# Later norms, two probability tiles, another PSUM pool for the output transposes, and a first attention without VectorE copies

## The chip, the cores and the metric

The kernel runs on one core of a Trainium2 chip. The metric is the device time of one execution in microseconds (us); the time given for a kernel is the median of its runs. TensorE is written PE (and PEld for its weight loads), VectorE DVE, ScalarE ACT, GpSimd POOL, and SyncE, which issues the DMAs here, SP.

## The reference, cut to what matters

The input is 16 sequences of 256 tokens with 128 channels. There are two parts, each behind a layer norm without weights and with a residual around it.

```python
x = x + first_attention(layernorm(x))     # windows of 64 tokens, 16 heads of 8
x = x + six_layers(layernorm(x))

def first_attention(x):
    q, k, v = split(x_windows @ W_qkv)                 # per head
    q, k = layernorm8(q) * g + b, layernorm8(k) * g + b
    return softmax(q @ k.T) @ v @ W_proj + b_proj

def six_layers(x):                         # windows of 32, look back one; 16 heads of 64
    for i in range(6):
        h = shift_tokens(x)
        q, k, v = split(h @ Wqkv[i])
        q, k = rotary(l2norm(q) * qs[i]), rotary(l2norm(k) * ks[i])
        x = local_attention(q, k, v) @ Wo[i] + x
        h = layernorm(shift_tokens(x)) * g[i] + b[i]
        a, gate = split(h @ W1[i] + b1[i])
        x = a * gelu(gate) @ W2[i] + b2[i] + x
    return x
```

`l2norm` divides each head's 64 values by the root of their squares' sum; `layernorm8` works over the 8 values of a head.

## The kernel before

**Order.** The kernel is a Python program that emits instructions; a planner then orders the instructions of each engine by when it believes that they are ready, with the order of the program as priority. In the six layers PE's order is pinned: `mul` and `flip` (L290 to L294) chain each matmul and transpose behind the one before, so PE runs them as the program emits them, and the others follow. All DMAs touched here are issued by SP, in order.

**First attention (L297 to L547).** Eight units of 512 tokens go through six stages, two steps `k` for a unit, one stage of several units side by side in each step (`merge`). `stage_load` (L364) takes row statistics (`row_stats`, L315: four sums and four sums of squares on ACT, for each of the unit's four tiles) and transposes. `stage_qkv` (L381) projects and normalises q and k. `stage_heads` (L406) splits q and k into a high and a low half-precision part, laid out four times eight values per head: ACT casts the high part (L414), POOL subtracts to get the low part (L415), and DVE copies both into the other two places (L417, L419); then SP transposes the block by DMA (L421). `stage_soft` (L427) makes scores, takes off the maximum on DVE (L448, L449), exponentiates (L459), splits again (L461 on ACT, L462 on POOL) and transposes by DMA (L464). `stage_out` (L467) multiplies probabilities with v for each half `c` of the partitions, into a PSUM tile `po` of its own, takes a reciprocal (L482) and two multiplies (L485) per half, and projects. `stage_norm` (L510) writes the residual to memory and takes the statistics for the second norm by the same `row_stats`. `SPLIT0` (L34) deals the eight PSUM banks to five pools.

**Six layers (L549 to L935).** There are 192 tiles (six layers, 32 tiles of 128 tokens). Each step `t` projects tile `t` (`stage_p`, L632) and does the later stages of tiles before it; `merge_at` (L248) sorts the pieces by their places within the step. `stage_p` has six projections: k in two halves, q in two halves, v in two halves. For a half of k or q DVE multiplies the projection with the rotary table (L643), ACT squares it (L652), DVE sums the squares per head (L653) and POOL adds the rotated parts (L654). After the second half ACT takes logarithm and exponential (L658, L659, through `tab`, whose line in the profile is L275), POOL clips (L660) and multiplies both halves (L664). In the next step PE transposes these halves, four to a bank (`turned`, L608; `project` calls `turn` between its matmuls), and ACT copies them out (L621). The probabilities of a tile go the same way, into one tile `pt` of which there is one buffer; `stage_v` (L765) reads it, in two halves `mb`. PSUM is dealt by `SPLIT` and `USE` (L33, L35): two banks for projections ("p"), four for transposes, feed-forward and more ("t", "w", "f", and half of `stage_v`), two for scores and the other half of `stage_v`. The feed-forward `stage_f` (L837) covers four tiles and is spread over four steps; its gelu needs another table of ACT's, so `tab` and `gelu` (L274, L280) order it against the logarithms and exponentials that come before. In the last layer `emit_out` (L820) transposes the result back, adds the residual of the first part and writes out; it takes its two banks from "p".

Of the kernel before, what the change touches and what calls it, by code (L numbers as in the profile page):

```python
# [33 lines left out]
SPLIT0 = (2, 2, 2, 1, 1)  # L34
# [14 lines left out]
VPRE = 16.0  # L49
# [6 lines left out]
def kernel(  # L56
# [240 lines left out]
    def first_attention(p1, p2, p3, pqp, psp0, pop, pyp, ptp=None):  # L297
# [17 lines left out]
        def row_stats(xt, pre):  # L315
# [3 lines left out]
            for t in range(4):  # L319
                S.activation(sq, xt[:, t], AF.Copy, scale=-1.0 / 128.0, accum_out=mu[:, t : t + 1])  # L320
# [43 lines left out]
        def stage_load(u):  # L364
# [5 lines left out]
            V.tensor_scalar(e.rv, e.rs, VPRE, None, ALU.mult)  # L370
# [35 lines left out]
        def stage_heads(u):  # L406
            e = U[u]
            e.hl = []
            for s in range(2):
                src = e.qk[:, :, s * 128 : s * 128 + 128].rearrange("p t (h d) -> p t h d", d=8)  # L410
                hl = p1.tile([128, 4, 16, 4, 8], HP, name=f"hl{s}")
                for t in range(4):
                    hi, lo = hl[:, t, :, 0], hl[:, t, :, 2 if s else 1]
                    S.copy(hi, src[:, t])  # L414
                    G.tensor_tensor(lo, src[:, t], hi, ALU.subtract)  # L415
                    if s:
                        V.tensor_copy(hl[:, t, :, 1:4:2], hl[:, t, :, 0:3:2])  # L417
                    else:
                        V.tensor_copy(hl[:, t, :, 2:4], hl[:, t, :, 0:2])  # L419
# [47 lines left out]
        def stage_out(u, n2):  # L467
            e = U[u]
            for n in range(2):
# [4 lines left out]
                for c in range(2):  # L474
                    r = slice(64 * c, 64 * c + 64)
                    po = pop.tile([128, 8, 18], F32, name="po")
                    for gm in range(8):
                        p = gm % 4 * 2 + gm // 4
                        for q, (a, b) in enumerate(((0, 0), (0, 1), (1, 0))):
                            T.matmul(po[:, p], pt0[r, a * 8 + gm], v[r, b, p], start=(q == 0), stop=(q == 2))  # L480
                    rc = p3.tile([128, 8], F32, name="rc0")
                    V.reciprocal(rc, po[:, :, 16])  # L482
                    for hp in range(2):
                        h = slice(64 * hp, 64 * hp + 64)
                        V.tensor_tensor(  # L485
                            o0[h, c],
                            po[h, :, hp * 8 : hp * 8 + 8],
                            rc[h].unsqueeze(2).to_broadcast([64, 8, 8]),
                            ALU.mult,
                        )  # L490
# [117 lines left out]
    def turned(src, dst, mb):  # L608
        hold = []

        def one(m):
            if m == 0:
                hold.append(bank("t").rearrange("p (m q) -> p m q", q=128))
            flip(hold[0][:, m], src(m), ident)
            if m == 3:
                to = dst
                if isinstance(dst, Tl):
                    if mb == 0:
                        dst.pt = work.tile([128, 8, 128], F32, name="pt", bufs=1)
                    to = dst.pt  # L620
                S.copy(to[:, mb * 4 : mb * 4 + 4], hold[0])  # L621
# [10 lines left out]
    def stage_p(t):  # L632
        d = tiles[t]
        tq = tqs[d.i]
        d.nat = {}
        for s in (1, 0):
            r = front.tile([128, 16], F32, name="r", bufs=3)
            mcs = []
            for hb in range(2):
# [11 lines left out]
                sq = front.tile([128, 8, 64], F32, name="sq")  # L651
                S.activation(sq, pp.rearrange("p (h d) -> p h d", d=64), AF.Square)  # L652
                V.tensor_reduce(r[:, hb * 8 : hb * 8 + 8], sq, AX.X, ALU.add)  # L653
                G.tensor_tensor(mc, m2[:, :, 0], m2[:, :, 1], ALU.add)  # L654
                mcs.append(mc)
                if hb == 0:
                    yield
            tab(r, r, AF.Ln, bias=tiny)  # L658
            tab(r, r, AF.Exp, scale=-0.5)  # L659
            G.tensor_scalar(r, r, 1e12 / WPRE, None, ALU.min)  # L660
            for hb in range(2):
                mc = mcs[hb]
                rb = r[:, hb * 8 : hb * 8 + 8]
# [4 lines left out]
        for hb in range(2):  # L668
# [5 lines left out]
            if hb == 0:  # L674
                yield
# [346 lines left out]
```

## Time and profile before

| what | value |
|---|---|
| median of three runs | 3215.65 us (3214.28 to 3218.32) |
| profiled execution | 3213.12 us, span 3211.3 us |
| PE busy | 2994.2 us, 93% |
| DVE busy | 2583.3 us, 80% |
| POOL busy | 2510.2 us, 78% |
| ACT busy | 2384.4 us, 74% |
| first projection of the six layers | starts at 268.8 us |

Everything in the profile comes from one profiled execution. Its page gives busy time by engine, the span in 40 slices of 80 us with a digit for the busy tenths, and the costliest groups of instructions. A group is named by line, engine and operation and by what it writes and reads (out<-in); after the bar come busy time, the mean length of one in ns, and the engine's idle time before them with what ended it. A line of the waits reads: engine and instruction that waited, what it waited for, total us, how often, the longest. A matmul's end is modelled, so a busy PE isn't PE at its peak.

### The profile page before, as it was taken

What the parts mean: (1) busy time and instruction counts of PE and PEld (TensorE: products, weight loads), DVE (VectorE), ACT (ScalarE), POOL (GpSimd) and SP (SyncE); (2) the same over time, 40 slices, a digit from 0 to 9 for tenths busy, and PEclk for the clock granted to TensorE, in tenths of its full rate; (3) what the DMA queues carried; (4) which work ended last, traced back from release to release, by engine and by line L of the source; (5) the groups of instructions that cost most, each with busy time, mean ns of one, the idle gap of its engine ahead of it and who ended that gap; (6) DMA issues with size and microseconds to landing.
All of it is one profiled execution on the core that took longest, in us unless ns stands there. A gap on an engine that the chain in (4) does not pass through costs nothing. (4 is left out here: it accounts for less than half of the span.)

```text
span 3211.3 us, 153330 instructions
## 1 busy us (share of the span) xinstructions
PE 2994.2 (93%) x67106; PEld 2099.0 (65%) x67106; DVE 2583.3 (80%) x4850; ACT 2384.4 (74%) x5034; POOL 2510.2 (78%) x2578
## 2 busy tenths in 40 slices
PE   4887999999999999999999999999999999999997
PEld 3655766666666666666666666666666666666664
DVE  7987888887788887788887788887788887787774
ACT  6877777777777777777777777777777777776774
POOL 5656988888888788888788888788888788887772
PEclk6558999999999999999999999999999999999998
DMA  4763545444444434444444444444444444443433
GB/s 109 134 130 86 101 96 106 89 85 88 93 95 107 87 87 88 93 95 105 89 87 86 94 96 104 89 88 84 95 98 103 89 89 81 95 93 91 89 89 71
DMA packets 622945, 302.98 MB, mean 94 GB/s; under 512 B 533446, under 2 KB 545732, under 8 KB 622276
## 3 DMA queue, kind: packets, MB, share of 16 engines
q1 hardware_dynamic: 622276, 293.18, 43.5%
q8 instruction: 528, 8.65, 1.1%
q14 instruction: 141, 1.16, 0.1%
HBM read 22.45 MB, written 4.19 MB: 8 GB/s over the span
## 5 line engine op out<-in xcount | busy, mean ns | idle before, releaser
L291 PE MATMUL bank<-wqkv,xhl 128*128 128x512 f16 x3456 | 1234.4, 380 | 10.0 <-ACT sq L652 9.3
L654 POOL TENSOR_TENSOR sum<-mc 128x512 f32<-128x512 f32 x768 | 995.8, 1300 | 230.4 <-DVE mc L643 211.3
L643 DVE TENSOR_TENSOR mc<-bank,tq 128x1024 f32<-128x1024 f32 x768 | 928.2, 1218 | 148.3 <-PE bank L294 135.4
L664 POOL TENSOR_TENSOR sum<-sum,r 128x512 f32<-128x512 f32 x768 | 796.2, 1058 | 31.9
L653 DVE TENSOR_REDUCE r<-sq 128x8 f32<-128x512 f32 x768 | 520.4, 683 | 277.4 <-ACT sq L652 267.4
L294 PE MATMUL bank<-ident,sum 128*128 128x128 f32 x3072 | 710.5, 273 | 0.0
L796 POOL TENSOR_TENSOR ohl<-of,ohl 128x512 f16<-128x512 f32 x384 | 451.7, 1176 | 211.5 <-ACT ohl L795 210.8
L652 ACT ACTIVATE sq<-bank 128x512 f32<-128x512 f32 x768 | 459.6, 608 | 160.4 <-DVE mc L643 158.7
L294 PEld LDWEIGHTS bank<-ident,sum 128*128 128x128 f32 x3072 | 432.4, 141 | 131.8 <-issue 13.9
L291 PEld LDWEIGHTS <-xhl 128*128 128x128 f16 x3456 | 337.6, 98 | 191.0 <-issue 18.5
L795 ACT CAST ohl<-of 128x512 f16<-128x512 f32 x384 | 237.8, 619 | 269.5 <-DVE of L791 266.8
L291 PE MATMUL bank<-vb,pt 64*32 64x65 f32 x6144 | 376.0, 225 | 50.9 <-ACT p L275 26.4
L291 PEld LDWEIGHTS bank<-vb,pt 64*32 64x32 f32 x6144 | 257.0, 105 | 218.6 <-ACT p L275 75.1
L294 PE MATMUL bank<-ident,p 128*128 128x128 f32 x1536 | 355.0, 273 | 0.1
L291 PE MATMUL bank<-v,pt 64*32 64x65 f32 x6144 | 312.6, 224 | 39.4 <-ACT p L275 17.8
L291 PE MATMUL bank<-vw,pt 64*32 64x65 f32 x12288 | 331.8, 225 | 1.2 <-issue 1.0
L791 DVE TENSOR_TENSOR of<-bank,rc 128x256 f32<-128x256 f32 x768 | 295.4, 416 | 1.7
L291 PE MATMUL bank<-ot,wohl 128*128 128x128 f16 x4608 | 292.0, 220 | 2.0 <-issue 1.1
L291 PEld LDWEIGHTS bank<-kt,qt 64*32 64x32 f32 x24576 | 255.4, 105 | 44.4 <-issue 44.1
L291 PE MATMUL bank<-kt,qt 64*32 64x64 f32 (+1 forms) x24576 | 283.7, 223 | 0.3 <-issue 0.2
L291 PEld LDWEIGHTS bank<-v,pt 64*32 64x32 f32 x6144 | 235.2, 105 | 70.5 <-ACT p L275 33.2
L291 PEld LDWEIGHTS <-wohl 128*128 128x128 f16 x4608 | 259.1, 98 | 21.0 <-issue 3.1
(155 smaller groups left out, 5033.9 us busy)
## 6 DMA issues: line engine op xcount, KB each, us to landing
v<-vb SPq DMA_DIRECT2D x384, 130.0 KB
vw<-vb SPq DMA_DIRECT2D x384, 130.0 KB
vw<-vb SPq DMA_DIRECT2D x576, 65.0 KB
wraw<-in_L_ffn_Wqkv_dram SPq DMA_DIRECT2D x36, 256.0 KB
wraw<-in_L_ffn_Wo_dram SPq DMA_DIRECT2D x12, 256.0 KB
ot<-ohl SPq DMA_TRANSPOSE x192
xt<-in_L_attn_x_dram SPq DMA_DIRECT2D x8, 256.0 KB
r1d<-xt SPq DMA_DIRECT2D x8, 256.0 KB
```

The lines of the kernel that those rows point to most:

```text
L291: pin(T.matmul(*args, **how))
L294: pin(T.transpose(*args))
L643: V.tensor_tensor(prod, p4.unsqueeze(3).to_broadcast([128, 8, 2, 2, 32]), tq[:, s, d.j].unsqueeze(1).to_broadcast([128, 8, 2, 2, 32]), ALU ...
L652: S.activation(sq, pp.rearrange("p (h d) -> p h d", d=64), AF.Square)
L653: V.tensor_reduce(r[:, hb * 8 : hb * 8 + 8], sq, AX.X, ALU.add)
L654: G.tensor_tensor(mc, m2[:, :, 0], m2[:, :, 1], ALU.add)
L664: G.tensor_tensor(mc, mc, rb.unsqueeze(2).to_broadcast([128, 8, 64]), ALU.mult)
L791: V.tensor_tensor(of[:, :, a], po[a][:, :, 0:64], rc.unsqueeze(2).to_broadcast([128, 4, 64]), ALU.mult)
L795: S.copy(ohl[:, 0, h], of)
L796: G.tensor_tensor(ohl[:, 1, h], of, ohl[:, 0, h], ALU.subtract)
```

## The change

It has four parts.

First attention: ACT casts and POOL subtracts with an input that is read twice, so each writes two of the four places, and the DVE copies go. The output matmuls of both halves `c` alternate and write one tile of two banks, with one reciprocal and two multiplies for both. The second row statistics take their means by one DVE reduction and a small POOL multiply; a scaling of four numbers (`rv`) goes from DVE to POOL. The pool of `po` has one buffer of two banks instead of two of one.

Norms: the squares of both halves go into one tile, one DVE reduction sums them, and it is emitted with the logarithm, the exponential and the POOL multiplies after the next projection's instructions.

Probabilities: `pt` is two tiles of four blocks each.

Output: `emit_out` takes its banks from "t".

```diff
-SPLIT0 = (2, 2, 2, 1, 1)
+SPLIT0 = (2, 2, 1, 1, 1)
...
-            for t in range(4):
-                S.activation(sq, xt[:, t], AF.Copy, scale=-1.0 / 128.0, accum_out=mu[:, t : t + 1])
+            if pre == "a":
+                for t in range(4):
+                    S.activation(sq, xt[:, t], AF.Copy, scale=-1.0 / 128.0, accum_out=mu[:, t : t + 1])
+            else:
+                V.tensor_reduce(mu, xt, AX.X, ALU.add)
+                G.tensor_scalar(mu, mu, -1.0 / 128.0, None, ALU.mult)
...
-            V.tensor_scalar(e.rv, e.rs, VPRE, None, ALU.mult)
+            G.tensor_scalar(e.rv, e.rs, VPRE, None, ALU.mult)
...
+                hi, lo = (slice(0, 2), slice(2, 4)) if s else (slice(0, 3, 2), slice(1, 4, 2))
                 for t in range(4):
-                    hi, lo = hl[:, t, :, 0], hl[:, t, :, 2 if s else 1]
-                    S.copy(hi, src[:, t])
-                    G.tensor_tensor(lo, src[:, t], hi, ALU.subtract)
-                    if s:
-                        V.tensor_copy(hl[:, t, :, 1:4:2], hl[:, t, :, 0:3:2])
-                    else:
-                        V.tensor_copy(hl[:, t, :, 2:4], hl[:, t, :, 0:2])
+                    two = src[:, t].unsqueeze(2).to_broadcast([128, 16, 2, 8])
+                    S.copy(hl[:, t, :, hi], two)
+                    G.tensor_tensor(hl[:, t, :, lo], two, hl[:, t, :, hi], ALU.subtract)
...
+                both = pop.tile([128, 2, 512], F32, name="po")
+                po = both[:, :, 0:144].rearrange("p c (m e) -> p c m e", e=18)
+                for gm in range(8):
+                    p = gm % 4 * 2 + gm // 4
+                    for q, (a, b) in enumerate(((0, 0), (0, 1), (1, 0))):
+                        for c in range(2):
+                            r = slice(64 * c, 64 * c + 64)
+                            T.matmul(po[:, c, p], pt0[r, a * 8 + gm], v[r, b, p], start=(q == 0), stop=(q == 2))
+                rc = p3.tile([128, 2, 8], F32, name="rc0")
+                V.reciprocal(rc, po[:, :, :, 16])
+                for hp in range(2):
+                    h = slice(64 * hp, 64 * hp + 64)
+                    V.tensor_tensor(
+                        o0[h],
+                        po[h, :, :, hp * 8 : hp * 8 + 8],
+                        rc[h].unsqueeze(3).to_broadcast([64, 2, 8, 8]),
+                        ALU.mult,
+                    )
...
-                    if mb == 0:
-                        dst.pt = work.tile([128, 8, 128], F32, name="pt", bufs=1)
-                    to = dst.pt
-                S.copy(to[:, mb * 4 : mb * 4 + 4], hold[0])
+                    dst.pt[mb] = work.tile([128, 4, 128], F32, name=f"pt{mb}", bufs=1)
+                    S.copy(dst.pt[mb], hold[0])
+                else:
+                    S.copy(dst[:, mb * 4 : mb * 4 + 4], hold[0])
...
+        late = []
+
+        def norm(r, sq, mcs):
+            V.tensor_reduce(r, sq, AX.X, ALU.add)
+            tab(r, r, AF.Ln, bias=tiny)
+            tab(r, r, AF.Exp, scale=-0.5)
+            G.tensor_scalar(r, r, 1e12 / WPRE, None, ALU.min)
+            for hb, mc in enumerate(mcs):
+                rb = r[:, hb * 8 : hb * 8 + 8]
+                G.tensor_tensor(mc, mc, rb.unsqueeze(2).to_broadcast([128, 8, 64]), ALU.mult)
+
         for s in (1, 0):
             r = front.tile([128, 16], F32, name="r", bufs=3)
+            sq = front.tile([128, 16, 64], F32, name="sq", bufs=2)
...
-                sq = front.tile([128, 8, 64], F32, name="sq")
-                S.activation(sq, pp.rearrange("p (h d) -> p h d", d=64), AF.Square)
-                V.tensor_reduce(r[:, hb * 8 : hb * 8 + 8], sq, AX.X, ALU.add)
+                S.activation(
+                    sq[:, hb * 8 : hb * 8 + 8], pp.rearrange("p (h d) -> p h d", d=64), AF.Square
+                )
                 G.tensor_tensor(mc, m2[:, :, 0], m2[:, :, 1], ALU.add)
                 mcs.append(mc)
-                if hb == 0:
-                    yield
...
+                while late:
+                    norm(*late.pop())
+                yield
+            late.append((r, sq, mcs))
             d.nat[s] = mcs
-            yield
...
+            while late:
+                norm(*late.pop())
             if hb == 0:
                 yield
...
-                        mul(po[a][q, m], d.pt[r, mm, q], vv[s, a][r, mm], start=True, stop=True)
+                        mul(po[a][q, m], d.pt[mb][r, m, q], vv[s, a][r, mm], start=True, stop=True)
...
-            pm = bank("p")[:, 0:256].rearrange("p (t c) -> p t c", c=64)[:, 0:n]
+            pm = bank("t")[:, 0:256].rearrange("p (t c) -> p t c", c=64)[:, 0:n]
```

More of the change, by code (lines that the diff above doesn't have):

```diff
@@ L473, in stage_out @@
                 o0 = p3.tile([128, 2, 8, 8], F32, name="o0")
[L474 to L490, printed above, removed]
+                both = pop.tile([128, 2, 512], F32, name="po")
[16 more added lines that the diff above has]
+                    )
                 yield
@@ L615, in one @@
             if m == 3:
-                to = dst
                 if isinstance(dst, Tl):
-                    if mb == 0:
-                        dst.pt = work.tile([128, 8, 128], F32, name="pt", bufs=1)
-                    to = dst.pt
-                S.copy(to[:, mb * 4 : mb * 4 + 4], hold[0])
+                    dst.pt[mb] = work.tile([128, 4, 128], F32, name=f"pt{mb}", bufs=1)
+                    S.copy(dst.pt[mb], hold[0])
+                else:
+                    S.copy(dst[:, mb * 4 : mb * 4 + 4], hold[0])
         turns.extend((lambda m=m: one(m)) for m in range(4))
@@ L650, in stage_p @@
                 m2 = prod.rearrange("p h f g d -> p h f (g d)")
-                sq = front.tile([128, 8, 64], F32, name="sq")
-                S.activation(sq, pp.rearrange("p (h d) -> p h d", d=64), AF.Square)
-                V.tensor_reduce(r[:, hb * 8 : hb * 8 + 8], sq, AX.X, ALU.add)
+                S.activation(
+                    sq[:, hb * 8 : hb * 8 + 8], pp.rearrange("p (h d) -> p h d", d=64), AF.Square
+                )
                 G.tensor_tensor(mc, m2[:, :, 0], m2[:, :, 1], ALU.add)
                 mcs.append(mc)
-                if hb == 0:
-                    yield
[L658 to L663, printed above, removed]
-                G.tensor_tensor(mc, mc, rb.unsqueeze(2).to_broadcast([128, 8, 64]), ALU.mult)
+                while late:
+                    norm(*late.pop())
+                yield
+            late.append((r, sq, mcs))
             d.nat[s] = mcs
-            yield
         d.vb = vb = vbs[t % NV]
@@ L701, in line_up @@
             d = tiles[t - LAG_P]
+            d.pt = [None, None]
             for mb in range(2):
```

## The prediction

> **What bounds the kernel now.** I read the page's engine totals and 40 slices first, then engine busy by stretch, then each engine's waits.
>
> ```profile
> span 3211.3 us, 153330 instructions
> PE   4887999999999999999999999999999999999997
> DVE  7987888887788887788887788887788887787774
> PEclk6558999999999999999999999999999999999998
> ```
>
> The kernel has two parts. In the first slices (first attention) PE has gaps and its granted clock is about half; after that PE is full. Busy time by stretch (columns PE, PEld, DVE, ACT, POOL, clock, DMA share, GB/s):
>
> ```profile
> 60.00:180.00 120.00, 95.73 (x1632) 72.81 (x1630) 111.19 (x281) 91.40 (x256) 79.77 (x63) 0.51 0.69 129
> 180.00:270.00 90.00, 73.84 (x1246) 54.21 (x1243) 68.66 (x191) 63.22 (x179) 44.20 (x40) 0.50 0.63 120
> 340.00:3150.00 2810.00, 2697.44 (x62047) 1887.41 (x62046) 2283.18 (x4151) 2108.37 (x4285) 2290.46 (x2336) 1.00 0.44 93
> ```
>
> From 60 to 180 us DVE is busy 93%, ahead of PE (80%) and ACT (76%). Over 60 to 270 us DVE works 179.9 of 210 us and the rows of its waits there add up to 23.7: it is the engine that hardly ever rests, so it sets the pace of the first part. Part of that work is stretched. The window around 163 us shows it (start, length, engine):
>
> ```profile
> 162.52 2.13 POOL L462 TENSOR_TENSOR ph<-p,ph 128x1024 f16<-128x1024 f32 x1
> ...
> 163.06 1.68 DVE L419 COPY hl<-hl 128x256 f16<-128x256 f16 x1
> ```
>
> The copy's shortest run is 168 ns; this one took 1.68 us and ended (164.74) just after POOL's instruction did (164.65). The groups of 0 to 300 us (busy, mean ns | idle before):
>
> ```profile
> L485 DVE TENSOR_TENSOR o<-po,rc 64x64 f32<-64x64 f32 x128 | 28.0, 219 | 1.9
> L415 POOL TENSOR_TENSOR hl<-qk,hl 128x128 f16<-128x128 f32 x64 | 25.2, 431 | 2.5 <-ACT hl L414 2.5
> L417 DVE COPY hl<-hl 128x256 f16<-128x256 f16 x32 | 14.5, 468 | 0.2
> L419 DVE COPY hl<-hl 128x256 f16<-128x256 f16 x32 | 13.3, 449 | 5.3 <-POOL hl L415 5.2
> L482 DVE RECIPROCAL rc<-po 128x8 f32<-128x8 f32 x64 | 12.6, 200 | 9.1 <-PE po L480 8.3
> ```
>
> From 340 to 3150 us PE works 96%, and what it still waits for is named:
>
> ```profile
> PE bank L291 <- ACT p L275: 44.2, 166, 2.9
> PE bank L291 <- ACT gt L281: 22.4, 88, 0.3
> PE bank L291 <- ACT pt L621: 21.1, 46, 0.5
> PE bank L294 <- DVE gt L834: 9.4, 6, 1.6
> ```
>
> None of them is the norm. So an edit counts in the main part only where it moves one of these.
>
> **The change part by part.** The sum is against the profiled execution, 3213.1 us (span 3211.3 and 1.8 around it); the median of the runs, 3215.65, lies 2.5 above it.
>
> 1. *First attention, DVE.* Removed: the copies, 14.5 + 13.3 = 27.8 us; 32 of 64 reciprocals, 6.3; 128 multiplies of 64x64 (28.0) become 64 of 64x128, which by the 64x128 row of L817 (about 280 ns) are 17.9, so 10.1; the eight L370 scalings (mean 518 ns), 4.1. Added: eight reductions for the mean, by the 128x512 row of L448 (684 ns) 5.5. Net 27.8 + 6.3 + 10.1 + 4.1 - 5.5 = 42.8 us less DVE work.
>
> On POOL, L415 goes from 128 to 256 elements: rows of 431 ns at 128 and 1176 at 512 (L796) give 1.94 ns an element, so 248 ns x 64 = 15.9 us, plus 16 small ones of 245 ns (L660), 3.9. POOL has 124 of 210 us busy there and takes 20 more; without that cover all 20 would be paid. On ACT the wider cast costs 64 x 107 ns = 6.8 (slope of 294 ns at 128 to 1040 at 1024), and 32 sums of 304 + 191 ns go, 15.8: 9 less.
>
> How much of 42.8 reaches the end? With some 40 off, DVE falls to 140 in that stretch and PE leads with 169.6; PE's weight loads wait a further 19.6 there for the probabilities' transposes, whose number is unchanged. 170 + 19.6 = 189 instead of 210: **21 us**. Bounds: 0 if PE and the transposes already hold the stage, 42.8 if every DVE microsecond counts. I take 21 because PE's row is the nearest next limit.
>
> Its new waits: the attention output now has one two-bank tile, so PE waits for one reciprocal and two multiplies (0.2 + 2 x 0.28 = 0.76 us) of the tile before, with the next scores behind it. Between 0.3 (today's row of PE waiting for L485) and 31 x 0.76 = 24; I take 0, for such groups lie about 6.1 us apart (L525 starts from 113.7 to 285.5 us for eight units: 24.5 a unit, four groups each). The mean now passes DVE and POOL, where a 2.13 us L462 can stand ahead: up to 0.68 + 2.13 + 0.25 - 4 x 0.30 = 1.9 us later, with ACT's exponentials queued behind; 8 x 1.9 = 15 above, -9 below (ACT's saving), 0 taken, as ACT rests 26% there. The L370 scaling behind such an L462 holds L392, L393 and PE's next projection, but on DVE it already ran up to 1521 ns. SP's transposes of hl are released by POOL's last subtraction instead of a later copy; no DMA is added and none changes its place in SP's queue.
>
> The Trainium skill speaks against this: its page GPSIMD Engine Reference, section Engine selection, says that two-input elementwise work belongs on VectorE, GpSimd being about 2x slower. By unstretched copies (64 x 0.17 = 11 us) against 15.9 us more on POOL the move would lose 5 us if the two were equally loaded. The row decides for me: the copies cost 27.8 and POOL has room.
>
> The halves of the output matmuls now alternate between partitions 0-63 and 64-127. The Trainium skill's page TensorEngine Tiling (Array Packing), section Key Properties, says that such tiles run in parallel; by that up to half of L480's 51.7 us of PE, an estimate, would go too. No run here shows it. My sum has nothing for it.
>
> 2. *Norms one projection later.* Per pair of halves two reductions of 683 ns become one of 1210 (the 128x1024 row of L399): 384 x 0.156 = 60 us less DVE work, and DVE's 267.4 us of waiting for L652 goes. On the path this is 0, for PE is at 96% and waits for neither; without that cover it would be the whole gain. POOL's queue already has the multiplies of k (L664) behind the addition of q's first half (this L654), so the later place in the program moves them little:
>
> ```profile
> 1409.89 1.27 POOL L654 TENSOR_TENSOR sum<-mc 128x512 f32<-128x512 f32 x1
> 1411.12 0.25 POOL L660 TENSOR_SCALAR r<-r 128x16 f32<-128x16 f32 x1
> 1411.46 2.05 POOL L664 TENSOR_TENSOR sum<-sum,r 128x512 f32<-128x512 f32 x2
> ```
>
>  What is late next is the logarithm on ACT. It waits for the reduction today, with the gelu's table load queued behind it:
>
> ```profile
> 1414.31 0.31 ACT L275 ACTIVATE r<-r,tiny 128x16 f32<-128x16 f32 x1 [0.81 <-DVE r L653]
> 1414.65 0.22 ACT L275 ACTIVATE r<-r 128x16 f32<-128x16 f32 x1
> 1414.88 1.28 ACT L281 ACT_TABLE_LOAD   x1
> ```
>
> The combined reduction ends 1.21 - 0.69 = 0.52 us later after the second square. That happens in the 46 feed-forward blocks where PE waits for L281: +24 at most. Below, -20: half of the 44.2 that PE waits for L275, if DVE runs ahead. But DVE has 0.16 us (2 x 0.683 - 1.21) to 0.69 us (the first half's reduction) less to do upstream in the same step, more than 0.52 at its best, so I take a quarter of 24, **+6**.
>
> 3. *Probabilities in two tiles.* The copy L621 of the next tile follows PE's flips, which follow the last read on PE itself; the 21.1 us wait for L621 is for a bank of the pool of four. 0, both ways.
>
> 4. *Output transposes in the pool of four.* The wait for L834 (six times, 9.4 us): in a pool of four neither half needs the other's add. **-9.4**; Ends: that, 0 if a later bank of the pool waits in its place, +9.4 if the two extra tiles in its rotation cost as much again.
>
> Sum: -21 + 6 - 9.4 = -24.4. 3213.1 - 24.4 = 3188.7 for the profiled execution; from the median 3215.65 - 24.4 = **3191 us**.
>
> **Rivals.**
> *A, slower: the norm really comes a projection later in POOL's queue.* In one step the q multiply starts at 1447.75 and lasts 1.04; PE's flip of it starts at 1450.77:
>
> ```profile
> 1447.75 2.05 POOL L664 TENSOR_TENSOR sum<-sum,r 128x512 f32<-128x512 f32 x2
> ```
>
> That leaves 1.98 us. A projection slot is 2.5 (projections start from 268.8 to 3148.3 us, 192 tiles of six); with 0.52 it is 3.0, so PE stalls 1.0 us in one step of four: 47 x 1.0 = +48. 3215.65 - 21 - 9.4 + 48 = 3233. It decides from a delay of 1.98 + 30.4/47 = 2.6 us. For: POOL is 82% busy there. Against: the order noted above.
> *B, no change: first attention is held by PE and the transposes.* For: PE 94% in 180 to 210 us at clock 0.5, DMA 0.69. Then 3215.65 + 6 - 9.4 = 3212. Against: PE's own waits there name DVE's L449.
> *C, faster: all DVE time counts and the norm costs nothing:* 3215.65 - 42.8 - 9.4 = 3163. For: DVE's 98% with waits. Against: PE's 169.6.
>
> **How the numbers follow.** Forecast 0.50, own range 3172 to 3208; A 0.20, B 0.14, C 0.16. 0.2% (6.4 us) is about what a measurement of this kernel tells from no change. Faster: 0.49 + 0.16 + a third of B = 0.70; same 0.10; slower 0.20. The range runs from a little below C to A, 3157 to 3233.
>
> **What would show it.** L417 and L419 gone; the first projection, at 268.8 us today, some 20 us earlier, DVE's share in 60 to 180 us below PE's; the L834 wait gone; the L275 and L281 waits within a few us of 44.2 and 22.4. Wrong would be: the first projection where it was (B), PE's flips waiting for L664's successor (A), or new bank waits from another order on ACT.

## The result: 3228.6 us, 0.44% slower

The median of five runs is 3228.61 us (3227.84 to 3231.55), against 3215.65 us for the kernel before beside it. The ratio is 1.0044, with a 95% interval of 1.0029 to 1.0058: the change costs 9 to 19 us where a gain of 24 was forecast. The profiled execution took 3231.55 us, its span 3229.8; it is the longest of the five, so the two profiles lie 18.5 us apart where the medians lie 13.0.

The same lines of the page after, and the busy time by stretch (columns PE, PEld, DVE, ACT, POOL, clock, DMA share, GB/s):

```profile
span 3229.8 us, 152190 instructions
PE   4778999999999999999999999999999999999997
DVE  6887887887788787788787788887788787777774
PEclk9759999999999999999999999999999999999998
```

```profile
60.00:180.00 120.00, 91.87 (x1745) 67.09 (x1741) 100.41 (x211) 95.67 (x245) 88.76 (x73) 0.75 0.76 140
180.00:270.00 90.00, 66.39 (x1160) 44.59 (x1159) 68.11 (x132) 62.73 (x151) 56.69 (x54) 0.57 0.61 111
340.00:3150.00 2810.00, 2672.15 (x61308) 1865.71 (x61307) 2246.29 (x3736) 2095.16 (x4243) 2263.47 (x2308) 1.00 0.44 91
```

From 60 to 180 us DVE is down from 111.2 to 100.4 us and POOL up from 79.8 to 88.8, as the diff says. From 340 to 3150 us DVE works 37 us less, and PE too works 25 us less in the same time: it is idle more often. Where the two parts begin and end is read from the group of the projections (count; shortest, median and longest ns; first to last start). Before:

```profile
L291 PE MATMUL bank<-wqkv,xhl x3456: 376/379/634, 268.8 to 3148.3; 128*128 128x512 f16 x192
```

After:

```profile
L291 PE MATMUL bank<-wqkv,xhl x3456: 376/379/634, 252.7 to 3164.8; 128*128 128x512 f16 x192
```

First attention ends 16.1 us earlier. From the first to the last projection there are now 2912.1 us instead of 2879.5, 32.6 more. What follows the last projection went from 63.0 to 65.0 us. The sum, -16.1 + 32.6 + 2.0, is the 18.5 us between the two spans. Engine busy time over exactly those projections says what the 32.6 consist of. Before:

```profile
268.80:3148.30 2879.50, 2757.42 (x63354) 1927.93 (x63351) 2342.30 (x4247) 2160.45 (x4407) 2355.35 (x2405) 1.00 0.43 93
```

After:

```profile
252.70:3164.80 2912.10, 2763.94 (x63367) 1928.06 (x63361) 2329.97 (x3861) 2168.34 (x4407) 2353.04 (x2401) 1.00 0.43 91
```

PE's idle time (length less busy) grew from 122.1 to 148.2 us, 26 of the 32.6; the rest is busy time. Its waits from 340 to 3150 us after, to be set beside those shown of before:

```profile
PE bank L291 <- ACT p L275: 71.6, 240, 0.6
PE bank L291 <- ACT gt L281: 31.5, 92, 0.4
PE bank L291 <- ACT pt L620: 16.4, 36, 0.5
```

The wait for ACT's attention exponential (L275, tile p) was 40.6 us in that stretch before (the 44.2 of the prediction is the row from 340 to 3170 us), now 71.6; that for the gelu was 22.4, now 31.5. The wait for L834 is gone, as forecast. So ACT is late. What ACT itself waits for ahead of its logarithm (tile r), before:

```profile
ACT r L275 <- DVE r L653: 151.2, 206, 1.8
ACT r L275 <- POOL sum L654: 13.0, 16, 0.8
ACT r L275 <- DVE rc L790: 5.0, 17, 0.3
```

After:

```profile
ACT r L275 <- DVE r L640: 218.3, 196, 2.8
ACT r L275 <- DVE rc L800: 76.2, 139, 0.8
ACT r L275 <- POOL sum L667: 46.0, 33, 1.9
```

That is 169 us in 239 waits before and 341 us in 368 after: of 384 logarithms, nearly every one now waits. Counted over the timeline of the whole profile, where k's and q's take turns, k's logarithm waited 64 times of 192 for 20.8 us before and 190 times for 106.2 after, q's 180 times for 151.5 us and 192 times for 246.5. A piece of the timeline shows both kinds of logarithm, k's and q's (start, length, engine; in brackets the idle time before and its releaser). Before, q's waited 0.81 us in the line that the prediction shows; a k of the kernel before waited for nothing:

```profile
1394.19 0.31 ACT L275 ACTIVATE r<-r,tiny 128x16 f32<-128x16 f32 x1
```

After, k's and q's of one step, with the reduction that q's waits for:

```profile
1394.56 0.31 ACT L275 ACTIVATE r<-r,tiny 128x16 f32<-128x16 f32 x1 [0.39 <-DVE rc L800]
...
1400.16 0.31 ACT L275 ACTIVATE r<-r,tiny 128x16 f32<-128x16 f32 x1 [1.35 <-DVE r L640]
```

```profile
1398.85 1.22 DVE L640 TENSOR_REDUCE r<-sq 128x16 f32<-128x1024 f32 x1 [1.03 <-ACT sq L664]
```

q's wait is 1.35 instead of 0.81 us, 0.54 longer, and k's, which mostly did not wait, now does. DVE stands idle for 1.03 us ahead of the combined reduction: it has nothing left to do and waits for the second square. The work that the combined reduction saves is saved in a pause there (such pauses stand ahead of 175 of the 384).

ACT's order changed as well. The planner sets it, and with the new norms it set it differently. In the same step as the first of these logarithms, the kernel before has the cast of the attention output (tile ohl) behind the two exponentials p:

```profile
1390.31 0.59 ACT L621 COPY kt<-bank 128x512 f32<-128x512 f32 x1 [0.20 <-PE bank L294]
1390.80 1.09 ACT L275 ACTIVATE p<-bank 128x512 f32<-128x512 f32 x2
1391.76 0.63 ACT L795 CAST ohl<-of 128x512 f16<-128x512 f32 x1
```

After, it stands ahead of them:

```profile
1390.62 0.62 ACT L805 CAST ohl<-of 128x512 f16<-128x512 f32 x1 [0.32 <-DVE of L801]
1391.14 0.58 ACT L622 COPY kt<-bank 128x512 f32<-128x512 f32 x1
1391.62 1.09 ACT L275 ACTIVATE p<-bank 128x512 f32<-128x512 f32 x2
```

Between 300 and 3120 us the cast stands ahead of both exponentials in 90 of 187 steps before, and in 140 of 185 after.

### The profile page after: what moved, and what is told of

Same layout as the page of the kernel before. It is cut to its first block, busy times and chain, and to the rows that moved or that the text cites. A ratio compares the mean times of both kernels' runs of the same rounds, so it can differ in the third digit from the quotient of the medians.

```text
span 3229.8 us, 152190 instructions
## 1 busy us (share of the span) xinstructions
PE 2982.5 (92%) x67106; PEld 2080.9 (64%) x67106; DVE 2545.8 (79%) x4306; ACT 2388.9 (74%) x4970; POOL 2528.6 (78%) x2594
## 5 line engine op out<-in xcount | busy, mean ns | idle before, releaser
L656 DVE TENSOR_TENSOR mc<-bank,tq 128x1024 f32<-128x1024 f32 x768 | 938.6, 1222 | 185.8 <-PE bank L294 158.1
L640 DVE TENSOR_REDUCE r<-sq 128x16 f32<-128x1024 f32 x384 | 466.9, 1216 | 201.5 <-ACT sq L664 195.3
L664 ACT ACTIVATE sq<-bank 128x512 f32<-128x512 f32 x768 | 468.6, 613 | 62.7 <-DVE mc L656 60.4
L275 ACT ACTIVATE r<-r,tiny 128x16 f32<-128x16 f32 x384 | 118.1, 308 | 352.4 <-DVE r L640 228.0
```

The lines of the kernel that those rows point to most:

```text
L275: made = S.activation(*args, **how)
L640: V.tensor_reduce(r, sq, AX.X, ALU.add)
L656: V.tensor_tensor(prod, p4.unsqueeze(3).to_broadcast([128, 8, 2, 2, 32]), tq[:, s, d.j].unsqueeze(1).to_broadcast([128, 8, 2, 2, 32]), ALU ...
L664: S.activation(sq[:, hb * 8 : hb * 8 + 8], pp.rearrange("p (h d) -> p h d", d=64), AF.Square)
```

## Experiments on the main part

The theory after these two profiles was that the norms' part loses what the rest gains and more, and in it the combined sum, whose longer wait on ACT reaches PE. The rivals: the rest of the change does not gain what was forecast; or the norm's later place delays it, as rival A of the prediction has it; or, of the combined sum, not its length counts but the missing second reduction or the shared tile. A further rival is ACT's changed order: no run lengthens k's sum and holds that order.

Each kernel was timed in five rounds beside the kernel before; a difference is that of the two medians, an interval that of the ratio.

| kernel | median, us | before, us | difference | 95% interval of the ratio |
|---|---|---|---|---|
| all but the norms | 3188.19 | 3212.51 | -24.3 | 0.9907 to 0.9934 |
| norms alone | 3254.19 | 3212.51 | +41.7 | 1.0113 to 1.0144 |
| late, two sums | 3214.51 | 3212.34 | +2.2 | 0.9994 to 1.0012 |
| one sum, old place | 3254.04 | 3212.34 | +41.7 | 1.0115 to 1.0146 |
| sums of 4 and 12 heads | 3237.22 | 3215.06 | +22.2 | 1.0057 to 1.0084 |
| one sum for q | 3221.80 | 3215.06 | +6.7 | 1.0012 to 1.0031 |
| one sum for k | 3234.10 | 3216.76 | +17.3 | 1.0041 to 1.0068 |
| two tiles and pool of four | 3200.87 | 3212.51 | -11.6 | 0.9951 to 0.9976 |
| two tiles alone | 3213.31 | 3212.34 | +1.0 | 0.9992 to 1.0010 |

### Is it the norms?

The change without its norms' part, and the kernel before with that part alone:

```diff
 # all but the norms: the kernel after, but stage_p as before
-            sq = front.tile([128, 16, 64], F32, name="sq", bufs=2)
...
+                sq = front.tile([128, 8, 64], F32, name="sq")
+                S.activation(sq, pp.rearrange("p (h d) -> p h d", d=64), AF.Square)
+                V.tensor_reduce(r[:, hb * 8 : hb * 8 + 8], sq, AX.X, ALU.add)
```

> The whole change except its norms: sums per half, logarithm, exponential and multiplies stand where they stood before. Theory N (the later, combined norm holds ACT's queue and so PE): the first part keeps its 16 us, the wait for L834 stays gone (9 us), and the six layers lose the rest of the loss: 3215.7 - 16 - 9 = 3190 (3184 to 3197). Theory P (another of the parts changed the order of the queues in the six layers, and the norms are innocent): the six layers stay 33 us longer than before, 3225 to 3232.

> The kernel before with the new norms alone. N: 42 us more than before (the 33 that the six layers grew by, and the 9 that the output transposes hid), 3257 (3245 to 3265), the first projection where it was at 269 us, PE's wait for L275 near 72 us. P: 3210 to 3222.

Without the norms' part the rest gains 24.3 us and beats both kernels; alone, the norms' part loses 41.7. In the profile with the norms alone PE's wait for L275 is where it is in the kernel after (stretch 340 to 3140 us):

```profile
PE bank L291 <- ACT p L275: 73.8, 244, 0.7
```

### Late, or combined?

The norms' part does two things: it emits the norm a projection later, and it sums both halves in one reduction. Each was done alone; the late one with two sums also keeps a tile of squares for each half.

```diff
 # late, two sums: as the norms alone, but
-            V.tensor_reduce(r, sq, AX.X, ALU.add)          # in norm()
...
+                V.tensor_reduce(r[:, hb * 8 : hb * 8 + 8], sq, AX.X, ALU.add)   # at each half
```

> The kernel before, with logarithm, exponential, clip and multiplies emitted one projection later, but the sums still made for each half where they were (683 ns each). Theory L (what costs is the length of the one sum over both halves, 1216 ns between the second square and the logarithm): the loss of 42 us is gone, 3212 (3205 to 3220), ACT's waits for the sum as before (168 us in all). Theory D (the later place in the program is what costs): 3245 to 3260, those waits near 340 us.

```diff
 # one sum, old place: the kernel before, but
+            sq = front.tile([128, 16, 64], F32, name="sq", bufs=2)
...
-                V.tensor_reduce(r[:, hb * 8 : hb * 8 + 8], sq, AX.X, ALU.add)
...
+            V.tensor_reduce(r, sq, AX.X, ALU.add)
             tab(r, r, AF.Ln, bias=tiny)
```

> The kernel before, with one sum over both halves right after the second half, everything else of the norm in its old place. L: the whole loss, 3254 (3245 to 3262), ACT's waits for the sum near 340 us. D: 3212 (3205 to 3220).

The late place costs nothing that can be measured (1.0003); the combined sum in its old place costs all 41.7. The two profiles, PE's waits from 340 to 3140 us; late with two sums:

```profile
PE bank L291 <- ACT p L275: 40.4, 162, 0.4
```

One sum in the old place:

```profile
PE bank L291 <- ACT p L275: 72.8, 241, 0.7
```

The first has the number of the kernel before, the second that of the kernel after. The order of ACT goes with them: the cast stands ahead of both exponentials in 90 of 187 steps with the late two sums, and in 140 of 185 with one sum in the old place.

### Is it the length of the last sum, and whose?

A combined sum is one longer instruction, but there is also one instruction less and a shared tile of squares. Dealing the 16 heads out as 4 and 12 keeps two reductions in their old places and changes their lengths; the squares of both halves lie in one shared tile, as with the combined sum.

```diff
+            sq = front.tile([128, 16, 64], F32, name="sq", bufs=2)
...
-                V.tensor_reduce(r[:, hb * 8 : hb * 8 + 8], sq, AX.X, ALU.add)
+                ws = slice(4, 16) if hb else slice(0, 4)
+                V.tensor_reduce(r[:, ws], sq[:, ws], AX.X, ALU.add)
```

> The kernel before with the sums of squares dealt 4 heads and 12 heads in place of 8 and 8: as many reductions, both in their old places, and the total length of the two stays at about 1.37 us, but the second, for which the logarithm waits, takes about 0.69 + 0.26 = 0.95 us. Theory L, the wait for the last sum is the whole loss of 41.7 us (0.53 us longer): about half of it, 3212 + 20 = 3232, with PE's wait for L275 near 55. If the loss comes from having one reduction instead of two (fewer pieces for the order of the engines to place, or the shared tile of squares): 3212 with nothing lost for the first, some loss with PE's wait still near 40 for the second.

The loss is 22.2 us, about half of 41.7, for a reduction that is half as much longer (groups from 340 to 3140 us; busy, mean ns | idle before):

```profile
L656 DVE TENSOR_REDUCE r<-sq 128x12 f32<-128x768 f32 x369 | 350.2, 949 | 175.0 <-ACT sq L652 169.5
L656 DVE TENSOR_REDUCE r<-sq 128x4 f32<-128x256 f32 x368 | 150.8, 410 | 100.6 <-ACT sq L652 90.8
```

```profile
PE bank L291 <- ACT p L275: 74.3, 210, 1.4
...
PE bank L291 <- ACT gt L281: 13.1, 45, 0.3
```

949 ns is 0.27 us over today's 683, the combined sum's 1216 ns are 0.53 over. At these two lengths, then, the time follows the length of the last sum; that this is by the wait alone is not shown. PE's single rows do not follow it in proportion: 74.3 for p instead of the expected 55, while the gelu's fell to 13.1. The row for p goes rather with ACT's order, in which the cast stands ahead of the second exponential in 141 of 186 steps here (in 50 of them between the two). PE's idle time over all has the whole price: 144.0 us from the first to the last projection, 22 over before's 122.1.

Then one sum for q alone, and for k alone:

```diff
+                if s or hb:                    # q alone; for k alone: if not s or hb
+                    ws = slice(hb * 8, hb * 8 + 8) if s else slice(0, 16)
+                    V.tensor_reduce(r[:, ws], sq[:, ws], AX.X, ALU.add)
```

> The kernel before with one sum over both halves for q only; k keeps its two. If the longer wait counts alike for k and q: 3212 + 21 = 3233. If only k counts, which is first in the step: 3212 to 3216. If only q counts, behind which the gelu and the projections of v stand: 3250 to 3254.

> The kernel before with one sum over both halves for k only; q keeps its two. One sum for both cost 41.7 us, for q alone 6.7. If the two add up: 35 us, about 3248. If the loss comes only from both together (each alone is covered by the other's slack): 3212 to 3222.

6.7 and 17.3 us. Neither lies where one of its theories had it, and the two do not add up to 41.7: they make 24.0, and 17.7 come only when both are long. These runs also answer for the shared tile: both have it for k and q, so it costs at most the 6.7 of the first. PE's wait for L275 from 340 to 3140 us tells them apart. q alone:

```profile
PE bank L291 <- ACT p L275: 42.0, 165, 1.0
```

k alone:

```profile
PE bank L291 <- ACT p L275: 72.8, 244, 0.6
```

So the wait for the attention exponentials comes with k's longer sum. With q's, ACT waits as much longer (92 us more ahead of q's logarithms in the run for q alone, 85 more ahead of k's in the run for k alone), and PE's row for p stays. The two runs differ in ACT's order too: for q alone the cast stands ahead of both exponentials in 90 steps, as before, for k alone in 141 of 186. In 51 more steps a cast of 0.62 us stands in front, 32 us by estimate, and PE's row for p grows by 32: the order can account for that row by itself. Whether k's sum costs by its length or by the order that the planner makes of it stays open. Of q's 6.7 us only 2.0 are idle time of PE (124.1 against 122.1 us from the first to the last projection), of k's 17.3 it is 16.6. Why the two together cost more than their sum stays open as well.

### The two tiles and the pool

```diff
 # two tiles and pool of four: first attention and norms as before, and
-                        mul(po[a][q, m], d.pt[r, mm, q], vv[s, a][r, mm], start=True, stop=True)
+                        mul(po[a][q, m], d.pt[mb][r, m, q], vv[s, a][r, mm], start=True, stop=True)
...
-            pm = bank("p")[:, 0:256].rearrange("p (t c) -> p t c", c=64)[:, 0:n]   # kept for two tiles alone
+            pm = bank("t")[:, 0:256].rearrange("p (t c) -> p t c", c=64)[:, 0:n]   # for two tiles and pool of four
```

> The kernel before with the probabilities in two tiles and the output transposes in the pool of four, nothing else. N: 3215.7 - 9 = 3206 (3203 to 3211), all of it in the last layer. P, if the two tiles or the banks changed the order of the queues: over 3220.

> The kernel before with the probabilities in two tiles alone, output transposes in the pool of two. If the two tiles do nothing, as PE's own order already spaces the copies: 3212.5 (3209 to 3216), and all the 12 us of the pair come from the pool of four. If they do help: 3207 or less.

The two tiles alone do nothing measurable, so the 11.6 us are the pool of four's by difference (it was not run alone); the time lies 2 us below the range that was expected. In its profile PE's wait for L834 is gone, and its first rows are those of before (340 to 3140 us), so nothing took its place:

```profile
PE bank L291 <- ACT p L275: 41.3, 165, 0.4
PE bank L291 <- ACT gt L281: 22.1, 87, 0.3
```

## Experiments on the first attention

| kernel | median, us | before, us | difference | 95% interval of the ratio | first projection, us |
|---|---|---|---|---|---|
| before | | | | | 268.8 |
| first attention's change alone | 3199.20 | 3212.51 | -13.3 | 0.9944 to 0.9969 | 251.8 |
| no DVE copies, alone | 3211.28 | 3212.34 | -1.1 | 0.9986 to 1.0004 | 268.6 |
| output stage alone | 3206.82 | 3212.92 | -6.1 | 0.9972 to 0.9989 | 258.9 |
| output stage, halves in turn | 3212.86 | 3212.92 | -0.1 | 0.9990 to 1.0008 | 264.6 |
| statistics alone | 3221.80 | 3212.92 | +8.9 | 1.0018 to 1.0041 | 272.9 |
| the scaling rv alone | 3209.39 | 3212.34 | -3.0 | 0.9980 to 0.9998 | 265.7 |
| no norms, DVE copies kept | 3195.12 | 3212.92 | -17.8 | 0.9930 to 0.9958 | 260.7 |
| no norms, old statistics | 3187.43 | 3212.34 | -24.9 | 0.9907 to 0.9934 | 255.2 |
| no norms, halves in turn | 3187.46 | 3212.34 | -24.9 | 0.9913 to 0.9940 | 253.8 |

The last three have the two tiles and the pool of four as well, so they stand beside "all but the norms" (-24.3, first projection at 250.5).

### The whole, and the copies

The first attention's change alone is the diff of the change from `SPLIT0` to the merged multiplies.

> The kernel before with the new first attention alone. N: 16 us less, 3200 (3194 to 3205), first projection near 253 us, the six layers as long as before (2880 us). P, if first attention is what changed the order of the queues: six layers 20 to 40 us longer, 3220 to 3240.

```diff
 # no DVE copies, alone: stage_heads as after, all else as before
-                    S.copy(hi, src[:, t])
-                    G.tensor_tensor(lo, src[:, t], hi, ALU.subtract)
...
+                    two = src[:, t].unsqueeze(2).to_broadcast([128, 16, 2, 8])
+                    S.copy(hl[:, t, :, hi], two)
+                    G.tensor_tensor(hl[:, t, :, lo], two, hl[:, t, :, hi], ALU.subtract)
```

> The kernel before, with the high and low parts written twice by ACT and POOL and no DVE copies; the rest of first attention as before. If DVE sets the pace and the copies' 27.8 us are the bulk of what it was freed of (42.8 us gave 13), 3212.5 - 13 x 27.8 / 42.8 = 3204 (3200 to 3209). If the gain came from the output's single tile and its alternating matmuls instead: 3210 to 3215.

A surprise: 27.8 us of DVE copies are gone, and the time stands still. DVE's busy time up to the first projection fell only from 219.5 to 211.2 us. Groups from 0 to 269 us; before:

```profile
L307 DVE TENSOR_SCALAR rqb<-sm 128x128 f32<-128x128 f32 x8 | 4.5, 557 | 0.0
L312 DVE TENSOR_SCALAR rqb<-rqb 128x128 f32<-128x128 f32 x8 | 1.7, 218 | 0.1
L516 DVE TENSOR_TENSOR bmu<-bmu,brs 128x4 f32<-128x4 f32 x7 | 1.6, 232 | 1.6 <-ACT brs L302 1.6
```

Without the copies (L516 is L513 there):

```profile
L307 DVE TENSOR_SCALAR rqb<-sm 128x128 f32<-128x128 f32 x8 | 7.1, 882 | 0.1
L312 DVE TENSOR_SCALAR rqb<-rqb 128x128 f32<-128x128 f32 x8 | 6.4, 795 | 0.1
L513 DVE TENSOR_TENSOR bmu<-bmu,brs 128x4 f32<-128x4 f32 x7 | 7.4, 1056 | 3.1 <-ACT brs L302 3.1
...
L416 POOL TENSOR_TENSOR hl<-qk,hl 128x256 f16<-128x256 f32 x64 | 40.5, 672 | 9.3 <-ACT hl L415 9.3
```

A multiply of four numbers that took 232 ns takes 1056 in the mean and 2079 at its longest, and that one ends with an instruction of POOL (191.27 and 191.25 us), as the copy of the prediction does:

```profile
189.13 2.12 POOL L459 TENSOR_TENSOR ph<-p,ph 128x1024 f16<-128x1024 f32 x1 [3.17 <-ACT ph L458]
189.19 2.08 DVE L513 TENSOR_TENSOR bmu<-bmu,brs 128x4 f32<-128x4 f32 x1 [0.22 <-ACT brs L302]
```

The copies' stretched time did not leave with them: with POOL busier (its subtraction has 40.5 us in place of 25.2), other DVE instructions are stretched instead, by 13.1 us in the three rows compared above. DVE's busy time still fell by 8.3 us, and the time did not; what holds the stage there was not traced. The Trainium skill's page Perfetto Trace Analysis, section Optimizing Scalar/DVE Operations, warns that DVE and GpSimd share a read port, "so offloading operations between those two might not help"; this run agrees, with -1.1 us for 27.8 us of copies; the port itself no run here shows.

### The output stage

```diff
 # halves in turn: merged tile, reciprocal and multiplies, but
-                for gm in range(8):
-                    p = gm % 4 * 2 + gm // 4
-                    for q, (a, b) in enumerate(((0, 0), (0, 1), (1, 0))):
-                        for c in range(2):
-                            r = slice(64 * c, 64 * c + 64)
+                for c in range(2):
+                    r = slice(64 * c, 64 * c + 64)
+                    for gm in range(8):
+                        p = gm % 4 * 2 + gm // 4
+                        for q, (a, b) in enumerate(((0, 0), (0, 1), (1, 0))):
```

> The kernel before with one part of the first attention's change: the output matmuls of both halves alternate and write one two-bank tile, with one reciprocal and two multiplies for both. The whole first attention's change gave 13.2 us (3212.5 to 3199.2), the copies alone 1.1. Theory O, the gain comes from the alternating matmuls, whose PE time fell from 51.7 to 34.2 us and whose weight loads fell from 44.6 to 27.0: about 3200. Theory D, it comes from DVE's merged reciprocals and multiplies (16.4 us less): also about 3200, but then the next kernel but one (halves in turn) has it too. Theory R, it comes from the row statistics: 3212. Theory S, it takes several parts together: 3206 to 3211.

> As the kernel with the output stage alone, but the 24 matmuls of one half run before the 24 of the other, as in the kernel before; the tile, the reciprocal and the multiplies stay merged. Theory O: 3212 or slower (3212 to 3220, as the merged tile now also waits for both halves), with 51 us of PE in these matmuls. Theory D: about 3200.

The merged DVE instructions alone give nothing, with the alternating halves it is 6.1 us. The group of these matmuls (PE busy, mean ns | idle), alternating in the kernel after and in turn in the run, within 0 to 253 and 0 to 269 us:

```profile
L482 PE MATMUL po<-v,pt 64*128 64x18 f16 x1536 | 34.3, 174 | 22.1 <-DMA pt<-ph 18.8 <-DVE o L487 3.3
```

```profile
L481 PE MATMUL po<-v,pt 64*128 64x18 f16 x1536 | 48.3, 173 | 14.5 <-DMA pt<-ph 14.4
```

One matmul takes 173 to 174 ns either way; alternating, their busy time together is 34.3 us instead of 48.3 in turn and 51.7 in the kernel before, so the two halves overlap.

### The statistics

```diff
 # statistics alone; "the scaling rv alone" has only the last line
+            if pre == "a":
+                for t in range(4):
+                    S.activation(sq, xt[:, t], AF.Copy, scale=-1.0 / 128.0, accum_out=mu[:, t : t + 1])
+            else:
+                V.tensor_reduce(mu, xt, AX.X, ALU.add)
+                G.tensor_scalar(mu, mu, -1.0 / 128.0, None, ALU.mult)
...
-            V.tensor_scalar(e.rv, e.rs, VPRE, None, ALU.mult)
+            G.tensor_scalar(e.rv, e.rs, VPRE, None, ALU.mult)
```

> The kernel before with the row statistics' part alone: the second norm's means by one DVE reduction and one small POOL multiply for each unit in place of four sums on ACT, and the small scaling on POOL in place of DVE. Theory R: about 3200. Theories O and D: 3212, within 2 us of before. Theory S: 3206 to 3211. The prediction took 0 from this part, between -9 and +15.

> The kernel before with the scaling of four numbers for each unit on POOL in place of DVE, nothing else. Of the 8.9 us that the new statistics cost alone: if the scaling behind POOL's 2.1 us instructions holds v and PE's next projection, 3217 to 3222; if it is the mean on DVE and POOL, 3212 to 3214.

The scaling on POOL gains 3.0 us, where no gain was expected, and both together lose 8.9, which none of the four theories had. So the means on DVE and POOL cost about 12 by difference; they were not run alone. ACT's wait for the POOL multiply in the run with both (30 to 273 us):

```profile
ACT sq L326 <- POOL bmu L324: 8.0, 3, 5.9
```

Only 4.1 of the 8.9 us lie ahead of the first projection. The rest lies in the main part, whose code is the same, and was not traced: the main part's length differs by some 9 us among kernels with that code (2875.2 us without the copies, 2884.1 here), and most of that is busy time of PE (2755.9 and 2762.2), not waiting.

### Which parts count beside each other

Four parts that alone give -1.1, -6.1 and +8.9 make -13.3 together. Three kernels leave one of them out, with the pool of four and the old norms in all.

```diff
 # no norms, DVE copies kept: stage_heads as before
 # no norms, old statistics: row_stats and rv as before
 # no norms, halves in turn: the output loop as in the diff above
```

> The kernel after without the norms' part and without the new writing of the split: the DVE copies of the kernel before are back, everything else of the first attention, the two tiles and the pool of four stay. With the new writing this kernel took 3188.2 us. If the copies are free also when the output stage is lighter (theories O and D): 3188 to 3190. If they only begin to cost once the output stage no longer holds the units (theory S): 3194 to 3200.

> The kernel after without the norms' part and with the row statistics of the kernel before. By themselves the new statistics cost 8.9 us. If that price holds beside the other edits: 3188.2 - 8.9 = about 3179, which would be the fastest of all. If it is only paid while the copies and the old output stage hold the units: 3188, within 3 us of the kernel with the new statistics. If the statistics help once DVE is relieved (they take 16 us of sums off ACT): 3192 to 3197.

> The kernel after without the norms' part, but with the halves' output matmuls in turn, so that PE keeps its 51 us there while all 43 us less DVE work stay. Theory T, DVE's relief counts only when PE is relieved too (PE and its waits already hold the first attention, the prediction's bound of 0): 3200 to 3206, as with the pool of four alone (3200.9). Theory V, DVE sets the pace and the copies need only the rest of DVE's relief beside them: 3188 to 3194.

Beside the other parts the copies are worth 6.5 us (-17.8 against -24.3), the statistics and the alternating halves nothing (-24.9 both). What the three fastest share is the pair "no copies" and "merged output on DVE", and neither of the two gains alone (-1.1 and -0.1). The theory that PE had to be relieved too falls, for with the halves in turn PE keeps its 51.5 us of output matmuls and the time is the same. That DVE's relief counts only when both of the stages that run side by side have it is argued from this, not shown: the pair was not run without both of the other edits, and which wait holds a unit while only one stage is relieved stays open. On that reading the alternating halves stand in for the missing relief in part (-6.1).

The fastest kernels are the three at 3187 to 3188 us, 0.8% below before: the change without its norms' part, with or without the new statistics and the alternating halves.

## Why the prediction was wrong

**Norms, +6: the step that failed.** Its size of the delay was right: "0.52 us later" measured 0.54. Its 0 for the saved DVE work stands: no run shows a gain from it. Wrong was where the delay counts: the prediction let it reach PE only "in the 46 feed-forward blocks where PE waits for L281: +24 at most", and took a quarter of that. The measured term is +41.7, above its upper end. Two readings were at fault.

First, PE's largest wait, 44.2 us for L275, names the exponential of the attention, which stands in ACT's queue with the logarithms. "None of them is the norm" was read from PE's rows alone; one engine further up, ACT's own rows show 169 us of waiting ahead of the norm's logarithm in 239 places. k's logarithm mostly did not wait before, and with the longer reduction it waits in 190 of 192 steps, not in one of four; the runs for k alone and q alone show that k's is the larger share. The prediction named "new bank waits from another order on ACT" as a sign of being wrong, and that sign came: the cast ahead of the attention exponentials in 140 steps instead of 90. Its sum has no term for it. How much of the 41.7 is this order and how much the wait itself stays open.

Second, the offset, "DVE has 0.16 us to 0.69 us less to do upstream in the same step". In the steps shown DVE idles for 1.03 us ahead of the combined reduction, and before it idled 0.89 us ahead of the second half's:

```profile
1413.53 0.69 DVE L653 TENSOR_REDUCE r<-sq 128x8 f32<-128x512 f32 x1 [0.89 <-ACT sq L652]
```

There the last square sets the start, and nothing that DVE does less of upstream makes it earlier; so it is in 175 of the 384 combined reductions. Some 58 us of work were indeed saved (768 x 683 ns = 524 us became 466.9), and the wait that was to go, 267.4 us for the square, is still 195.3:

```profile
L640 DVE TENSOR_REDUCE r<-sq 128x16 f32<-128x1024 f32 x384 | 466.9, 1216 | 201.5 <-ACT sq L664 195.3
L294 PE MATMUL bank<-ident,sum 128*128 128x128 f32 x3072 | 710.7, 273 | 2.2 <-POOL sum L646 1.4
```

The Trainium skill's page Perfetto Trace Analysis, in the same section, has the rule that speaks against this part: where Scalar or Vector are not saturated but cause bubbles on other engines, "breaking up instructions may allow work to be completed sooner". The combined sum does the reverse, and 41.7 us is its price here.

**Rival A** gave 3233 us, close to the time measured, but for a reason that did not occur. PE's flips wait 1.4 us in all for POOL's multiply (the second row above), and the later place by itself cost nothing measurable.

**First attention, -21: right in sign and too large; its reason held in part.** Measured alone it is -13.3, inside the bounds of 0 and 42.8. The prices of the single instructions held: the multiply of 64x128 at 287 ns for 280, the reduction for the mean at 672 for 684, the wider cast at 406 for 401, POOL's subtraction at 691 for 679. What failed is the sum "42.8 us less DVE work" with PE as the next limit: up to the first projection DVE's busy time fell by 25.8 us (219.5 to 193.7), for part of the stretch behind POOL's instructions moved to others, and DVE still leads from 60 to 180 us (100.4 against PE's 91.9), where the prediction wanted it below PE. Already its reading that DVE "hardly ever rests" was generous: 179.9 of 210 us is 86%, the waits beside it are rest, and from 180 to 270 us PE was busier than DVE (73.8 against 68.7 us). Two figures behind its rivals are off as well, without effect on the sum: DVE's 98% with waits is 97% by its own numbers, and the DMA share of 0.69 is that of 60 to 180 us, 0.60 from 180 to 210. Rival B (nothing gained) is what each of the two DVE parts does alone. Two terms were taken at 0 and are not: PE's wait for the merged tile is 3.3 us, and the new means cost about 12 alone, though nothing beside the rest. The loss of 5 us for the move to POOL, which the prediction estimated from its rows beside the Trainium skill's page GPSIMD Engine Reference (Engine selection), did not come either: -1.1 alone and -6.5 beside the rest.

**Tiles 0 and pool -9.4: right.** They measured +1.0, with the interval on both sides of none, and -11.6 for both.

**The sum.** With the measured terms it is -13.3 + 41.7 - 11.6 = +16.8; the kernel shows +13.0. Without the norms' part the measured terms give 3215.65 - 24.9, about 3191. That this is the number that was forecast is luck: the forecast without that part is -30.4, its first attention was too large by 8 us and its pool too small by 2.

## What to carry to other kernels

A reduction that is split so that its first part runs while the second part's input is made is shorter where its reader waits. Merging it saved busy time on an engine that idled there, and here 0.53 us of length cost 42 us of the whole. Where a planner sets the order, compare the order of the engine behind the longer instruction too, before the price is put down to the wait. When the bounding engine's waits name an instruction of another engine, read what that engine's queue waits for before pricing anything at nothing. And an engine's stretched instructions are no safe budget: taking them away here moved part of the stretch to others, while the engine that goes with it did more.

## What the runs showed of the hardware that was not expected

- The granted clock of PE in first attention does not set the time there. It was 0.51 from 60 to 180 us before and 1.00 in the run with the halves in turn (PEclk of that window), and the output matmuls took 173 ns in both, the 128x384 ones 559 and 570. Since a matmul's end is modelled, the times of whole runs weigh more: of the runs of the kernel before beside the late two sums, 20 with a mean clock below 0.965 have a median of 3213.2 us and six with 0.99 or more 3212.1.
- Matmuls of the two halves of the partitions overlap when they alternate: 34.3 us of busy PE in place of 48.3 in turn for the same 1536. The prediction had cited the Trainium skill for this (TensorEngine Tiling (Array Packing), section Key Properties) without a row of its own; here is the row. The time gained is 6 us alone and none beside the other edits.
- ACT's total waiting in the main part hardly grew with the change, it moved: the rows from 340 to 3150 us add up to 675 us before and 680 after. Two of them before:

```profile
ACT ohl L795 <- DVE of L791: 263.6, 231, 2.5
...
ACT sq L652 <- DVE mc L643: 148.7, 260, 1.5
```

After:

```profile
ACT ohl L805 <- DVE of L801: 153.9, 237, 2.3
...
ACT sq L664 <- DVE mc L656: 51.7, 133, 0.6
```

The waits ahead of the norm's logarithm (the rows for r, shown with the result) are 171 us longer, those for the attention output and the product with the rotary table 207 us shorter. Their sum hides the change here; where in its queue ACT idles shows it.
